# Two-layer graph attention on one core: raw weights of the pair scheme loaded one superblock sooner, raw-block sums on VectorE, fewer asides per pair, contexts of blocks 14 and 15 moved

## The chip, the cores and the metric

The kernel runs on one core of a Trainium2 chip. The metric is the device time of one execution in microseconds, the median of several runs. The engines are TensorE (PE in the profile, with its weight loads as PEld), VectorE (DVE), ScalarE (ACT), GpSimd (POOL) and SyncE (SP), which here issues nearly all DMAs. Each engine takes its instructions in program order and waits on semaphores.

## The reference, cut to what matters

The input is x of 128 graphs with 64 nodes and 768 features, and an adjacency of 128 x 64 x 64. All is float32.

```
h = max(layernorm(x), 0)
for l in 0, 1:
    u_left, u_right = h (W_left[l] h)^T / sqrt(768),  h (W_right[l] h)^T / sqrt(768)
    u = u_left on and above the diagonal, u_right below it (masked by the adjacency)
    att = exp(u) * adj, normalized over each row
    ctx = att @ (h W_lin[l]^T + b_lin[l])
    h = relu(layer_norm(ctx) * ln_a[l] + ln_b[l])
out = x + h
```

## The kernel before

**Tiling.** The 8192 rows are 16 blocks of 512 rows (8 graphs). Two blocks make a superblock, of which there are 8 (`NU`). A weight of 768 x 768 is cut into 3 x 3 raw blocks of 256 x 256, each one tile of 128 x 512 floats (256 KB). Products are not made block by block: a fast scheme for block matrices makes sums of raw weight blocks and sums of token blocks, multiplies those, and adds the results into the output blocks. For a superblock this scheme has 29 products instead of 36 (`PRODUCTS` for left and right weights, `PAIRS` for W_lin of layer 0). Its 23 weight sums stand in `W_OPS`; 9 of them have two raw blocks as operands (numbers below 9), the rest need other sums, two are sign changes. An older scheme with 15 products for a single block (`W_SUMS`, 17 weight sums, made in place from the raw blocks; `ORDER`) still serves the last two blocks of layer 0 and all of layer 1.

**Stages.** For each layer, `pass_one` makes the left and right products, scores and softmax (8 superblocks); `pass_two` makes the W_lin products (in layer 0: 7 superblocks by `pair`, then blocks 14 and 15 by `linear`, the last one in two halves), and from them and the softmax the contexts (`context`, `finish`). In the profile, pass one of layer 0 ends at about 901 us, the seven pairs run from 904 to 1305 us, blocks 14 and 15 until 1378 us.

**Order by hand.** There is no scheduler. `put(slot, f)` hangs work of the other engines on a numbered slot between TensorE's groups of matmuls: in pass one every product has four slots (116 in a superblock), in a pair two (58). `run(slot)` issues what hangs on a slot, and one item of the queue `idle`, the asides: only where nothing was given for the slot, or in every case where its second argument is true. `None` in `idle` is an empty place.

**The weights of the pair scheme** are made in the last superblock of pass one of layer 0 (there `run` takes an aside in each slot). `one_aside(0)` puts in order: 10 empty places, 9 loads of raw W_lin blocks (`load_n`: each load is led by a one-column marker, `paced`, a memset on DVE, which holds it until the tile is free), the centring of the blocks on DVE (`centre`), and `pair_weights`: 9 stores of raw blocks to memory (`keep`), 23 sums, which alternate between POOL and DVE, each with its store, then the 17 sums of the old scheme on POOL with stores, and the first 9 loads of streamed weights (`stream_n`). All this lies in one area of SBUF, `room`; sums whose last reader is done give their tile to a later sum. A pair's weight load is issued nine products ahead.

**The asides of pass two of layer 0** (`two_aside`) load the raw left and right blocks of layer 1, sum them on POOL and store them, in the shares that `pair` gives: for products with an odd number in both slots whatever is given, for even ones only in slots with nothing given.

**End of the pairs.** In the last pair `first_weights` loads the first six weights of the old scheme into the tile `xb` at slot 30. In `linear`, `ends` says behind which step of a block a context is made and in which slots its inverse and its two scalings follow (the scalings free the two PSUM banks `aux` for the next context).

**SP's queue** holds loads and stores of all kinds in program order; a store that waits for a sum holds all that stands behind it. The program numbers its DMAs around eight semaphores, so that a DMA waits for the one eight before it.

Of the kernel before, what the change touches and what calls it, by code (L numbers as in the profile page):

```python
# [17 lines left out]
def kernel(  # L18
# [12 lines left out]
    nc = tc.nc  # L31
# [70 lines left out]
    W = {}  # L102
# [158 lines left out]
    def pair_weights(own):  # L261

        where = {3 * i + j: single(s) for s, (i, j) in RAW.items()}
        spare = deque([single(s) for s in range(len(ORDER)) if s not in RAW] + own)
        last = {}
        for n, (_, o, _, a, b) in enumerate(W_OPS):
            for w in (a, b, o):
                last[w] = n

        def keep(w):  # L270
            if w in WN:
                nc.sync.dma_start(WN[w], where[w])

        def sums(n, eng):
            _, o, sign, a, b = W_OPS[n]
            t = where[o] = spare.popleft()
            if sign == "neg":
                eng.tensor_scalar_mul(t, where[a], -1.0)
            else:
                added(eng, t, sign, where[a], where[b])  # L280
            keep(o)
            for w in sorted({a, b, o}):
                if w >= 9 and last[w] == n:
                    spare.append(where[w])

        for w in range(9):
            idle.append(lambda w=w: keep(w))
        for n in range(len(W_OPS)):
            idle.append(lambda n=n: sums(n, (nc.gpsimd, nc.vector)[n % 2]))
        final = {s: -1 for s in range(len(ORDER))}  # L290
        for n, (o, *_) in enumerate(W_SUMS):
            final[o] = n

        def old(n):
            o, s, a, b = W_SUMS[n]
            added(nc.gpsimd, single(o), s, single(a), single(b))
            keep_old(n)

        def keep_old(n):
            for s in final:  # L300
                if final[s] == n:
                    nc.sync.dma_start(WO[s], single(s))

        idle.append(lambda: keep_old(-1))
        for n in range(len(W_SUMS)):
            idle.extend([lambda n=n: old(n), None])
        idle.append(None)
        for n in range(NR):
            idle.append(lambda n=n: stream_n(n))
# [634 lines left out]
    def pass_two(l, aside):  # L944
        last = l == L - 1
        with (tc.tile_pool(name=f"ps_two{l}", bufs=1, space=bass.MemoryType.PSUM) as ps,
# [154 lines left out]
            def pair(s, ends):  # L1101

                late, seen, bank = [], set(), {}
                HL[2 * s] = new_hl(2 * s)
                if not s:
                    HL[1] = new_hl(1)
                for i, (w, t, at, new, what) in enumerate(PAIRS):
                    if new:
                        bank[at] = ps_st.tile([P, 2 * TH], F32, name=at)
                    p = bank[at].rearrange("p (r d) -> p r d", r=2)  # L1110
                    x, wt = tokens(l, s, t, 2), single((s * len(PAIRS) + i) % NR)
                    for r in range(2):
                        for c in range(K2):
                            nc.tensor.matmul(p[:, r], x[:, c, r * P:(r + 1) * P], wt[:, c, :],  # L1114
                                             start=(new and r == c == 0), stop=(c == K2 - 1), skip_group_check=True)
                        if r == 0:
                            run(2 * i, i % 2)
                    now, late = late + [(p, what[n], int(what[n + 1], 16)) for n in range(0, len(what), 2)], []
                    for pp, sign, o in now:
                        u, j = 2 * s + o % 4 // 2, o // 4  # L1120
                        if u not in HL:
                            late.append((pp, sign, o))
                            continue
                        to = HL[u][:, o % 2 * 2:o % 2 * 2 + 2, j * D:(j + 1) * D]
                        if o in seen:
                            added(nc.vector, to, sign, to, pp)
                        else:
                            read_biased(pp, to, sign, j)
                        seen.add(o)
                    for o, last_i in LAST_PAIR.items():  # L1130
                        if last_i == i and o >= 12:
                            free((2, l, s, o))
                    n = s * len(PAIRS) + i + NR
                    if n < (NU - 1) * len(PAIRS):
                        stream_n(n)
                    else:
                        k = n - (NU - 1) * len(PAIRS)
                        nc.sync.dma_start(single(n % NR), WO[ORDER[6 + k][0]])
                        W[l, "n"][ORDER[6 + k][0]] = single(n % NR)
                    if i == 27 and s == NU - 2:  # L1140
                        AHEAD.append(fresh(l, 0, (0, 1)))
                    if i in ends:
                        what, slots = ends[i]
                        for f, n in zip(finish(*what), slots):
                            put(n, f)
                        if what[1] and what[0] == 2 * s - 2:
                            HL[2 * s + 1] = new_hl(2 * s + 1)
                    run(2 * i + 1, i % 2)
                assert not late

            def first_weights():
                t = sp.tile([P, H // 32, Q, 32], F32, name="xb", bufs=1).rearrange("p b q j -> p (b q j)")
                W[l, "n"] = {}
                for n in range(6):
                    to = W[l, "n"][ORDER[n][0]] = t[:, n * K2 * D:(n + 1) * K2 * D].rearrange("p (c d) -> p c d", c=K2)
                    nc.sync.dma_start(to, WO[ORDER[n][0]])

            def pairs():
                for s in range(NU - 1):
                    for n in range(2):  # L1160
                        put(4 + 10 * n, lambda n=n: load_h(2, l, 2 * s + 2 + n))
                        put(40 + 3 * n, lambda n=n: load_at(2 * s + n))
                    put_pair_ops(s, "after", PAIR_SLOTS)
                    if s + 1 < NU - 1:
                        put_pair_ops(s + 1, "before", PAIR_SLOTS)
                    else:
                        put_sums_t((2, l, NB - 2), 52, 1, 37)
                    for u, slot in ((NB - 5, 29), (NB - 4, 0)):
                        if u // 2 == s:
                            put(slot, lambda u=u: load_rows(1, u + 5 - NB, sp))  # L1170
                            put(slot + 1, lambda u=u, slot=slot: put_all(
                                slot + 14, transpose_rows(1, u + 5 - NB, sp), 1))
                    if s == NU - 2:
                        put(30, first_weights)
                    if s in aside:
                        aside[s]()
                    ends = {}
                    if s:
                        ends = {e: ((2 * s - 2 + n // 2, n % 2), (2 * e + 6, 2 * e + 7, 2 * e + 8))
                                for n, e in enumerate((0, 4, 9, 14))}  # L1180
                    pair(s, ends)
                    for n in sorted(plan):
                        plan[n - PAIR_SLOTS] = plan.pop(n)
                return NB - 2
# [35 lines left out]
            for u in range(0 if last else pairs(), NB):  # L1220
                turn = not last and u >= NB - 2
                put(12 if turn and u == NB - 2 else 4, lambda u=u: load_at(u))
                if u + 1 < NB:
# [9 lines left out]
                        aside[u]()  # L1233
                    ends = {}
                    if not last:
                        ends = {4 * n: ((u - 2 + n // 2, n % 2), (8 * n + 6, 8 * n + 7, 8 * n + 8)) for n in range(4)}
                    elif u:
                        ends = {0: ((u - 1, 0), (6, 7, 8, 11, 12)), 7: ((u - 1, 1), (20, 21, 22, 30, 30))}
                    linear(u, (0, 1), 0, ends, (0, 1) if u + 2 < NB else (0,))
# [2 lines left out]
                else:  # L1242
                    if turn:
                        put_token_ops(1, 0, "before")
                        assert not idle, len(idle)
                        for n in range(RINGS - 1):
                            put(20 + 4 * n, lambda n=n: stream(1, n))
                        ends = ({1: ((u - 1, 0), (13, 14, 16)), 11: ((u - 1, 1), (34, 35, 36))},
                                {4: ((u, 0), (50, 51, 52))})
                    else:  # L1250
                        last_block(u)
# [10 lines left out]
    def bias_aside(l):  # L1262
        def begin(sp):
            rows["bias", l] = bias(l)
        return begin

    def one_aside(l):
        def begin(sp):
            idle.extend(none * (8 if l else 10))
            later(load_n(l), 0)  # L1270
            centre(l)
            if l:
                later(sums_n(l), 0)
            else:
                own = sp.tile([P, 2 * H], F32, name="own", bufs=1)
                pair_weights([own[:, n * K2 * D:(n + 1) * K2 * D].rearrange("p (c d) -> p c d", c=K2) for n in range(3)])
# [60 lines left out]
```

## Time and profile before

| what | value |
|---|---|
| median of 3 runs | 2730.79 us (2730.25 to 2731.34) |
| the profiled execution | 2728.26 us, its span 2726.1 us |
| mean granted TensorE clock | 0.996 |
| TensorE matmul busy | 2682.3 us, 98% |
| VectorE, ScalarE, GpSimd busy | 1575.3, 746.2, 1465.9 us |
| DMA | 636.25 MB, mean 233 GB/s |

The profile gives for each instruction its start and duration in microseconds from the start of the span, and for the idle time before it the event that ended it. In a timeline, neighbouring instructions of one kind are one row with their number (x8). A row of a window gives the stretch, its length, the busy time of PE, PEld, DVE, ACT and POOL with the number of instructions, the granted TensorE clock, the busy share of the 16 DMA engines and GB/s.

### The profile page before, as it was taken

How to read it: one execution, taken by the hardware profiler on the slowest of the kernel's cores; microseconds unless marked ns; L12 is line 12 of the kernel's file. 1: busy time of each engine (PE TensorE's matmuls, PEld its weight loads, DVE VectorE, ACT ScalarE, POOL GpSimd, SP SyncE). 2: the span in 40 equal slices, each digit the busy share in tenths (PEclk: the TensorE clock that was granted, in tenths of full speed). 3: DMA queues.
4: the chain of work that ended last, by engine and by line, in shares of the span. 5: the costliest groups of instructions: out<-in, count | busy, mean ns of one | idle time of the engine just before them, and what ended most of it. 6: DMA issues, size and time to landing. Idle time of an engine off the chain costs nothing.

```text
span 2726.1 us, 47585 instructions
## 1 busy us (share of the span) xinstructions
PE 2682.3 (98%) x18458; PEld 2293.3 (84%) x18458; DVE 1575.3 (58%) x2575; ACT 746.2 (27%) x1334; POOL 1465.9 (54%) x1139
## 2 busy tenths in 40 slices
PE   9999999999998999999999999999999999999998
PEld 7888888888887888887688888888888888888886
DVE  7664655756747655555334645545446476666667
ACT  4032131231310022222531221221212204444443
POOL 5633244244337899766443335334243286887886
PEclk9999999999999999999999999999999999999999
DMA  8886966867768799879685967859659534655655
GB/s 269 269 309 207 297 200 210 274 202 242 257 219 292 258 340 351 314 248 302 207 267 181 301 208 241 247 202 301 201 194 313 196 101 126 179 160 163 177 161 149
DMA packets 347807, 636.25 MB, mean 233 GB/s; under 512 B 67008, under 2 KB 194240, under 8 KB 339392
## 3 DMA queue, kind: packets, MB, share of 16 engines
q1 hardware_dynamic: 347424, 632.82, 71.5%
q8 instruction: 148, 2.42, 0.4%
q14 instruction: 75, 0.61, 0.1%
q10 hardware_dynamic: 160, 0.39, 0.0%
HBM read 486.55 MB, written 146.54 MB: 232 GB/s over the span
## 4 chain that ended last, share of the span: by engine, by line
PE 90%; DVE 2%; POOL 2%; DMA 2%; issue 1%; ACT 1%; SPq 0%; DVEq 0%; POOLq 0%; ACTq 0%
PE right L628 16%; PE X L628 10%; PE V L628 10%; PE Z L628 8%; PE Y L628 8%; PE X L1200 7%; PE both L567 4%; PE V L1200 4%; PE Y L1114 3%; PE aux L974 3%; PE X L1114 3%; PE Y L1200 3%; PE Z L1114 3%; PE V L1114 3%; PE Z L1200 2%; POOL room L247 1%
## 5 line engine op out<-in xcount | busy, mean ns | idle before, releaser
L247 POOL TENSOR_TENSOR ts<-ht 128x512 f32<-128x512 f32 x303 | 418.1, 1385 | 103.1 <-PE right L628 48.5
L247 POOL TENSOR_TENSOR ts<-ht,ts 128x512 f32<-128x512 f32 x192 | 253.1, 1327 | 308.4 <-PE V L628 197.9
L628 PE MATMUL right<-ts,wp 128*128 128x252 f32 (+1 forms) x1632 | 381.2, 377 | 2.4 <-DVE m L247 1.8
L628 PEld LDWEIGHTS right<-ts,wp 128*128 128x128 f32 x1632 | 309.8, 190 | 42.2 <-DVE m L247 2.8
L247 POOL TENSOR_TENSOR ts<-ht,ht 128x512 f32<-128x512 f32 x191 | 243.8, 1284 | 170.9 <-PE right L628 92.7
L576 POOL TENSOR_TENSOR wm<-adj,tri 128x256 f32<-128x256 f32 x60 | 42.8, 735 | 476.2 <-DMA wp<-ws 370.0
L247 DVE TENSOR_TENSOR m<-m,X 128x512 f32<-128x512 f32 x160 | 105.4, 684 | 254.7 <-ACT m L398 166.3
L247 DVE TENSOR_TENSOR m<-m,right 128x504 f32<-128x504 f32 (+1 forms) x304 | 199.3, 673 | 86.6 <-PE right L628 73.6
L628 PE MATMUL Z<-ts,wp 128*128 128x256 f32 x992 | 234.4, 379 | 1.0 <-POOL room L247 1.0
L628 PEld LDWEIGHTS Z<-ts,wp 128*128 128x128 f32 x992 | 188.3, 190 | 26.2 <-POOL room L247 1.4
L628 PE MATMUL X<-ts,wp 128*128 128x256 f32 x872 | 207.5, 381 | 1.0 <-DVE wp L247 1.0
L628 PE MATMUL V<-ts,wp 128*128 128x252 f32 (+1 forms) x864 | 201.7, 377 | 0.0
L628 PEld LDWEIGHTS X<-ts,wp 128*128 128x128 f32 x872 | 164.4, 190 | 24.6 <-POOL ts L247 1.3
L628 PEld LDWEIGHTS V<-ts,wp 128*128 128x128 f32 x864 | 164.1, 190 | 20.8 <-DVE m L247 0.4
L475 ACT ACTIVATE ht<-ht,b_col,a_col 128x512 f32<-128x512 f32 x192 | 140.7, 803 | 138.6 <-DMA ht<-h 138.6
L398 ACT ACTIVATE m<-right 128x504 f32<-128x504 f32 (+1 forms) x64 | 36.1, 590 | 504.2 <-PE both L567 484.1
L1054 ACT ACTIVATE z<-aux 128x768 f32<-128x768 f32 x126 | 101.0, 807 | 230.8 <-PE aux L974 214.5
L1067 POOL TENSOR_TENSOR z<-z,b 128x768 f32<-128x768 f32 x62 | 112.7, 1830 | 89.8 <-DVE z L1064 89.8
L247 DVE TENSOR_TENSOR m<-m,Y 128x512 f32<-128x512 f32 x144 | 95.7, 683 | 109.8 <-PE Y L628 99.6
L247 POOL TENSOR_TENSOR ts<-ts,ht 128x512 f32<-128x512 f32 x110 | 141.5, 1287 | 13.8 <-PE V L628 8.3
L628 PE MATMUL right<-ht,wp 128*128 128x252 f32 (+1 forms) x624 | 146.2, 378 | 0.0
L247 DVE TENSOR_TENSOR m<-m,V 128x504 f32<-128x504 f32 (+1 forms) x160 | 104.4, 677 | 71.9 <-PE V L628 60.8
(264 smaller groups left out, 5128.3 us busy)
## 6 DMA issues: line engine op xcount, KB each, us to landing
wp<-ws SPq DMA_DIRECT2D x435, 512.0 KB, 6.3
ht<-h SPq DMA_DIRECT2D x62, 1536.0 KB, 8.5
room<-wn SPq DMA_DIRECT2D x203, 256.0 KB, 4.8
h<-room SPq DMA_DIRECT2D x112, 384.0 KB, 6.9
z<-z SPq DMA_DIRECT2D x128, 192.0 KB, 4.8
ws<-wp SPq DMA_DIRECT2D x93, 256.0 KB, 4.9
xr<-in_x_dram SPq DMA_DIRECT2D x120, 192.0 KB, 3.7
out_dram<-xr SPq DMA_DIRECT2D x120, 192.0 KB, 2.6
```

The lines of the kernel that those rows point to most:

```text
L247: (eng.tensor_add if sign == "+" else eng.tensor_sub)(o, a, b)
L398: nc.scalar.activation(to(o), p, AF.Copy, scale=1.0 if sign == "+" else -1.0)
L475: nc.scalar.activation(ht, ht, AF.Relu, bias=cols[1][:, c:c + 1], scale=cols[0][:, c:c + 1])
L567: nc.tensor.matmul(p[h * S + e:h * S + e + 32, q, e:e + 95], ht[:, c, b * S + e:b * S + e + 32], mb[:, e:e + 95], start=(c == 0), stop=(c ...
L576: nc.gpsimd.tensor_tensor(wm[:, :, k], adj[:, :, 1 - k], tri[:, k].unsqueeze(1).to_broadcast([P, Q, S]), op=ALU.mult)
L628: nc.tensor.matmul(p[:, g], wk[:, c, g * P:(g + 1) * P], tk[:, c, :].rearrange("p (b s) -> p b s", s=S)[:, :, :ns], start=(new and g == c ...
L974: nc.tensor.matmul(cx[k][i, m, :HH], at[j, q, :], hl[j, q, m * HH:(m + 1) * HH], start=True, stop=True)
L1054: nc.scalar.activation(zs[k].rearrange(two, n=2), cx[k], AF.Square, accum_out=ss[:, k:k + 1])
L1067: nc.gpsimd.tensor_add(zs[k], zs[k], rows["b"])
L1114: nc.tensor.matmul(p[:, r], x[:, c, r * P:(r + 1) * P], wt[:, c, :], start=(new and r == c == 0), stop=(c == K2 - 1), skip_group_check=True)
L1200: nc.tensor.matmul(p[:, n], b[t][:, c, r * P:(r + 1) * P], w[s][:, c, :], start=(i in FIRST and i not in PRELOAD and n == c == 0), stop=(c ...
```

## The change

1. The nine raw loads leave `one_aside(0)` and are put, one per slot, on slots 99 to 107 of the superblock before (`bias_aside`); the ten empty places go.
2. Of the 23 weight sums, the 9 with two raw operands go to DVE and the other 14 to POOL, each of the latter with an empty place behind it.
3. In a pair, every product gives an aside its second slot in any case, and its first slot if nothing is given there.
4. `first_weights` goes from slot 30 to slot 44 of the last pair; the dictionary it fills is made earlier.
5. In blocks 14 and 15: the inverse and the scalings of a context in block 14 come one slot sooner; in block 15 the context of the first half of block 14 is made behind step 3, not step 1, with its inverse and scalings four slots later.

```
@@ pair_weights
         for n in range(len(W_OPS)):
-            idle.append(lambda n=n: sums(n, (nc.gpsimd, nc.vector)[n % 2]))
+            raw = W_OPS[n][2] != "neg" and max(W_OPS[n][3:]) < 9
+            idle.append(lambda n=n, raw=raw: sums(n, nc.vector if raw else nc.gpsimd))
+            idle.extend(none * (not raw))
@@ pair
                         if r == 0:
-                            run(2 * i, i % 2)
+                            run(2 * i)
...
-                    run(2 * i + 1, i % 2)
+                    run(2 * i + 1, True)
@@ first_weights
-                W[l, "n"] = {}
@@ pairs
                     if s == NU - 2:
-                        put(30, first_weights)
+                        W[l, "n"] = {}
+                        put(44, first_weights)
@@ pass_two, blocks 14 and 15 of layer 0
-                        ends = {4 * n: ((u - 2 + n // 2, n % 2), (8 * n + 6, 8 * n + 7, 8 * n + 8)) for n in range(4)}
+                        ends = {4 * n: ((u - 2 + n // 2, n % 2), (8 * n + 5, 8 * n + 6, 8 * n + 7)) for n in range(4)}
...
-                        ends = ({1: ((u - 1, 0), (13, 14, 16)), 11: ((u - 1, 1), (34, 35, 36))},
+                        ends = ({3: ((u - 1, 0), (17, 18, 20)), 11: ((u - 1, 1), (34, 35, 36))},
                                 {4: ((u, 0), (50, 51, 52))})
@@ bias_aside
             rows["bias", l] = bias(l)
+            if l == 0:
+                put(98, lambda: put_all(99, load_n(l)))
@@ one_aside
-            idle.extend(none * (8 if l else 10))
-            later(load_n(l), 0)
+            if l:
+                idle.extend(none * 8)
+                later(load_n(l), 0)
             centre(l)
```

## The prediction

> **What bounds the kernel now.** I read the page's busy table first, then the waits of TensorE by stretch, then the timelines of TensorE, VectorE (DVE), GpSimd (POOL) and SyncE (SP) around each stretch that has waits.
>
> ```profile
> PE 2682.3 (98%) x18458; PEld 2293.3 (84%) x18458; DVE 1575.3 (58%) x2575; ACT 746.2 (27%) x1334; POOL 1465.9 (54%) x1139
> ```
>
> TensorE is the bound: 43.8 us of the 2726.1 us span are not matmul. From 160 to 795, 960 to 1270 and 1380 to 2240 us it hardly waits. So the change can give only what TensorE loses at the end of the first attention pass, the start and end of the pair stage, and the two linear blocks behind it.
>
> ```profile
> 846.71 3.25 PE L628 MATMUL Y<-ht,wp 128*128 128x256 f32 x8 [2.46 <-DVE m L247]
> 849.75 2.37 PE L628 MATMUL right<-ht,wp 128*128 128x256 f32 x8
> 903.94 2.40 PE L1114 MATMUL X<-room,ht 128*128 128x256 f32 x8 [2.42 <-DMA room<-wn]
> 906.13 3.19 PE L1114 MATMUL Y<-room,ht 128*128 128x256 f32 x8
> 936.11 1.99 PE L1114 MATMUL Y<-room,ht 128*128 128x256 f32 x8 [1.73 <-DMA room<-wn]
> 1286.20 2.37 PE L1114 MATMUL Z<-room,ht 128*128 128x256 f32 x8 [2.69 <-DMA room<-wn]
> 1296.86 1.97 PE L1114 MATMUL Y<-room,ts 128*128 128x256 f32 x8 [1.83 <-DMA room<-wn]
> 1326.51 1.51 PE L974 MATMUL aux<-hl,at 64*64 64x384 f32 x12 [0.63 <-ACT z L1072]
> ```
>
> Columns: start, length, instruction, idle time before it. An undisturbed group of eight matmuls starts 1.7275 us after the last (799.11 to 809.47: six groups in 10.36). I count what a stretch loses as its starts against this step, since a wait also slows what follows:
>
> ```profile
> 846.00:850.00 4.00, 3.29 (x9) 2.70 (x10) 2.33 (x4) 0.00 (x0) 4.00 (x3) 0.66 0.77 251
> 904.00:907.00 3.00, 3.00 (x11) 2.49 (x12) 2.86 (x5) 0.00 (x0) 2.92 (x3) 0.72 0.89 308
> 936.00:940.00 4.00, 3.89 (x18) 3.46 (x19) 1.42 (x3) 0.00 (x0) 2.13 (x3) 1.00 0.64 169
> ```
>
> The third number from the end is the granted clock: 0.66 and 0.72 behind waits of 2.46 and 2.42 us, 1.00 behind one of 1.73. So a wait above some 2.4 us costs about 1.8 more (846.71: 3.25-1.89 and 2.37-1.89; 903.94: 0.46+1.29 over the step). The Trainium skill, page "TensorE: Matmul & The Clock Gate", section "The HAM clock gate", puts the drop only behind an idle window of about 3.4 us. By that none of these waits would carry a surcharge, and some 5 us of the losses below would be unexplained. The rows decide.
>
> The losses: **A**, last superblock of pass one: 49 steps from 795.65 to 890.65 take 95.0 us where 84.65 are due, 10.35 lost. **B**, first pair: 2.42+0.46+1.29 at the start, 0.9 at 925, 2.0 at 936. **C**, last pair: 4.6 around 1286, 2.06 at 1296. **D**, blocks 14 and 15: 2.01 at 1325, 1.99 at 1335.6, 1.75 at 1344.8, 1.32 at 1365.3.
>
> **Part 1, loads a superblock sooner, raw sums on DVE (A).** The cause of A is order, not load:
>
> ```profile
> 829.31 1.27 POOL L247 TENSOR_TENSOR room<-room 128x512 f32<-128x512 f32 x1 [21.78 <-DVE room L243]
> 842.92 1.74 DVE L247 TENSOR_TENSOR room<-room 128x512 f32<-128x512 f32 x1 [3.74 <-POOL room L247]
> 885.32 14.26 SPq L302 DMA_DIRECT2D wo<-room x6
> 899.63 5.79 SPq L259 DMA_DIRECT2D room<-wn x9
> ```
>
> POOL sits 21.8 us behind the centring on DVE, because the W_lin blocks land only at 808 to 812. Then DVE and POOL wait for each other through sums that alternate, with the token sums and the reads of PSUM queued behind. After the change the nine loads are issued at slots 99 to 107 of the superblock before, about 758 to 766, where SP is nearly empty. Their 2.3 MB delay ring loads of 512 KB that are issued five to eight products (17 to 27 us) before use, which hides it. The nine markers on DVE before them wait for the store of block 15, issued 745.6 to 750 and landed 6.9 later, by 757: some 0 to 0.5. Centring moves into 773 to 806, where DVE now idles 15.6 us. The nine raw sums depend on no sum of POOL. The other fourteen go to POOL, one per two slots: two more there, two fewer on DVE. With the empty places added and dropped, the asides of this superblock are 116 for 116 slots instead of 121, so the first loads of the pair stage are issued at slots 107 to 115 rather than partly after the last product; they wait for POOL's sums in either case, and cost nothing of their own.
>
> Is POOL fast enough? Slot s of this superblock lies at 781.7+0.864s. Its first sum is slot 35, 812. From there to its last old sum (slot 104) stand 50 adds and 2 masks. At 1.27 (alone) this ends at 877, at 1.45 for the 27 adds that share time with DVE sums at 882. It lags its slots by 5 to 10 us; token sums are issued 16 slots (13.8 us) ahead, so TensorE waits 0 to 2. DVE's sums take 1.592 at the median beside POOL (0.65 at least). Four of them between slots 57 and 60 are 6.4 us, and they reuse tiles whose stores land at about 831 to 834.5, just when needed: 0 to 1 of wait. I take 8.5 of 10.35 back, with ends of 6 and 10.3.
>
> A rule speaks against this part: the Trainium skill, "SBUF — State Buffer", section "Who interferes with whom", says that a DVE instruction with two SBUF inputs blocks against a POOL instruction that reads SBUF. The 1.592 agrees. If every POOL op paid 1.72 by it, the 50 would end at 899 and A would return nothing. The sum goes by 1.27 to 1.45, since after slot 61 DVE has only PSUM reads left.
>
> **Part 1 at the start of the pairs (B).** Scores end at 901.5 now, 891 to 895 after. The nine first weights are issued behind the last old sum (now 899.6, landed 903.8; nine issues take 5.8): after 877 to 882 they land between 881 and 892, so the 4.2 lost at 903.94 goes. But what follows hangs on another clock, which the change leaves as it is: DVE's softmax of block 14 ends 6.4 after the scores, eight att stores take 5.1 of SP, and only then comes the tenth weight (913.18). With DVE free of POOL it would be 4.9. The twelfth weight is queued behind a 1.5 MB token load and lands 11 us after the tenth is issued (3.0 MB now, 2.75 after, one raw load fewer in front): 21 to 22.7 after the scores, against 23.7 now, where TensorE would want it at 19.2. Step 16 likewise: 31.5 to 33 against 34.5. So B returns 1.0 to 3.5 of 7.1, mostly as waits below 2.4; I take 2.0.
>
> **Part 2, fewer asides per pair.** Loads, sums and stores of the layer-1 weights spread: stores end at pair step 121, not 97; the right raw loads move from steps 53 to 58 to steps 63 to 71, behind two token loads and among z stores. DMA is full there (0.97 to 1.06 busy from 1012 to 1070). Weight loads land with little to spare: step 8's of pair 2 at 1049.6 for a use at 1051.27. One or two 256 KB loads more in front (0.7 each at 360 GB/s) make waits of 0 to 1.5; elsewhere the pressure falls. I take 0.6 lost, ends 0 and 4.
>
> Stores and sums of the asides go to SP and POOL alone there, POOL being 82% busy (255 of 310 us), so nothing on TensorE's path waits for them but the weight loads.
>
> **Part 3, first linear weights at slot 44 (C).** Now six loads go out at 1287.85 for 3.04 us of SP, ahead of the weight issued 1290.99 that ends the 1.83 wait. Moved, that weight goes 3 us sooner: 2.06 gone. The 4.6 around 1286 stays: that weight was issued at 1279.81, before the six. They now go at about 1295.4, 4 to 8.8 to land, for a use at 1303.5: 0 to 0.7. C returns 1.3 to 2.1; I take 2.0.
>
> **Part 4, contexts (D).** One slot sooner lets the first scaling on ACT pass one PSUM read: the second scaling ends 0.76 sooner before 1325 and 0.75 before 1335 (its VectorE inverse doesn't move). In block 15 the context goes behind step 3, but the scaling now stands ahead of the read of X that step 2 needs: that read ends at 1344.6 to 1345.1 against 1343.8 wanted, so 0.9 to 1.3 lost for 1.75. D returns 0.5 to 3; I take 2.1.
>
> The dictionary made earlier is no instruction.
>
> **Sum.** 8.5+2.0-0.6+2.0+2.1 = 14.0. The profiled run took 2728.26 (span plus 2.2), 2.5 below the median of 2730.79; the saving is taken from the median: 2716.8.
>
> **Rivals.**
> 1. The stall moves: DVE waits for recycled tiles and POOL lags to 899. A returns 5, B 1.0, C 2, D 0.5, pairs lose 1: 7.5, 2723.3. For it: the stores land when needed. Against: POOL starts 17 us sooner.
> 2. Everything goes, the pair start too: A 10.3, B 7.1, C 2.1, D 4.5: 24, 2706.8. Against: the token load in the queue.
> 3. The other side: the weight stream in pairs 2 to 4 falls behind. A weight over 2.4 late costs the wait and 1.8 of clock, 4.2 or more. Five such places undo 20 and give 2730.8-14.6+21 = 2737. It decides from loads landing 4 us later than now (1.7 spare plus 2.4). For it: DMA full. Against: the bytes are the same and pair 1, with as many stores, has no wait today. A milder form, two or three places, gives 2725 to 2731.
> 4. The loads don't come sooner: excluded by the order of the queue, where they stand among ring loads 2 to 4 of the next superblock; C, D and the pairs' loss alone would give 2727.3.
>
> **Chances.** Forecast 0.60 (2711 to 2721), rival 1 0.15, rival 2 0.07, rival 3 0.16 (0.06 of it slower), rival 4 0.02. Same means within 0.2%, 2725.3 to 2736.3, which is about what a measurement can tell. Faster 0.83, same 0.11, slower 0.06. The range takes in rival 1 and the near ends of 2 and 3.
>
> **What would show it.** Right: room loads landed by 776; no POOL wait of 20 us in 800 to 830; the old sums done by 882; no TensorE wait on DVE m above 1 us in the last superblock; at the pair start no wait for step 0, but one of 1 to 2.4 us around steps 11 and 16; no wait before 1297's step; 1286's still there. Wrong: a POOL chain to 899, waits on wn in pairs 2 to 4, or a wait of the first linear steps on xb.

## The result and the profile after

The changed kernel takes 2722.8 us (median of 10 runs, 2721.65 to 2728.35) against 2731.18 for the kernel before beside it: a ratio of 0.9971, 95% interval 0.9962 to 0.9981. That is 7.9 us less (5.2 to 10.4). The forecast was 14.0 less, and its first rival 7.5. The profiled execution took 2723.55 us, its span 2721.7.

The busy table of the page after:

```profile
PE 2680.5 (98%) x18458; PEld 2294.8 (84%) x18458; DVE 1575.1 (58%) x2573; ACT 745.8 (27%) x1334; POOL 1468.3 (54%) x1141
```

TensorE's timeline after, those rows that have a wait of 0.4 us or more between 790 and 1350 us (start, length, instruction, idle time and what ended it):

```profile
847.13 3.68 PE L630 MATMUL Y<-ht,wp 128*128 128x256 f32 x8 [4.50 <-DVE m L247]
898.94 2.48 PE L569 MATMUL Z<-m,ht 128*32 128x95 f32 x108 [2.00 <-issue]
924.57 2.69 PE L1116 MATMUL Z<-room,ts 128*128 128x256 f32 x8 [3.24 <-DMA room<-wn]
1284.02 1.96 PE L1116 MATMUL Z<-room,ht 128*128 128x256 f32 x8 [1.46 <-DMA room<-wn]
1288.97 1.97 PE L1116 MATMUL X<-room,ht 128*128 128x256 f32 x8 [1.26 <-DMA room<-wn]
1321.36 1.51 PE L976 MATMUL aux<-hl,at 64*64 64x384 f32 x12 [0.43 <-ACT z L1074]
1331.19 1.51 PE L976 MATMUL aux<-hl,at 64*64 64x384 f32 x12 [0.43 <-ACT z L1074]
1339.34 1.10 PE L1202 MATMUL X<-xb,ts 128*128 128x256 f32 x4 [1.27 <-ACT hl L400]
1345.22 1.10 PE L1202 MATMUL X<-room,ts 128*128 128x256 f32 x4 [0.55 <-ACT hl L400]
```

The last superblock (A) is left with one wait. It is longer than any before, and with the slower clock behind it A still loses 6.4 us. The start of the pairs has no wait for its first weight any more, but in the scores before it a wait of 2.00 us stands instead of 0.66, and the one at step 11 grew from 0.35 to 3.24. These two rows before:

```profile
899.04 2.48 PE L567 MATMUL Z<-m,ht 128*32 128x95 f32 x108 [0.66 <-issue]
925.21 1.97 PE L1114 MATMUL Z<-room,ts 128*128 128x256 f32 x8 [0.35 <-DMA room<-wn]
```

The wait in front of 1297's step is gone. The contexts of block 14 wait 0.43 instead of 0.63, and their four-matmul groups no longer wait.

To set the terms of the forecast against the traces I cut the span at points that both kernels have: the first group behind the second scores of the last superblock (t0), the start of its final scores, the first context of the second pair, the first linear step, and the first group of layer 1.

| stretch, us | before | after | saved | forecast |
|---|---|---|---|---|
| A: last superblock from t0 | 100.37 | 96.44 | 3.9 | 8.5 |
| final scores and first pair | 68.01 | 68.78 | -0.8 | 2.0 |
| other pairs | 345.09 | 341.90 | 3.2 | 1.4 |
| blocks 14 and 15 | 73.12 | 72.31 | 0.8 | 2.1 |
| sum | | | 7.2 | 14.0 |

The rest of the span is 2.8 longer in the execution after: 1.9 of it before t0, 0.9 behind the last stretch, where the change does nothing. The nine raw loads now lie before t0, but they are no clear price: t0 is 791.1 to 796.6 in the eight traces with early loads, and 792.1 to 794.9 in the four without.

**Where A's wait comes from.** By "the rings" I mean the 16 DMA engines with what is queued for them; how busy they are stands in the rows of a window. SP's queue after the change, around the wait, two rows of it:

```profile
824.48 1.24 SPq L470 DMA_DIRECT2D ht<-h  x1
829.62 0.32 SPq L272 DMA_DIRECT2D wn<-own  x1
```

and the chain of waits after the change, traced back from the end of this stretch (start, length, what):

```profile
829.62 10.71 DMA wn<-own
840.33 0.03 issue
840.36 0.02 DVEq L247
840.38 0.04 issue
840.42 4.39 DVE own L247 x3
844.81 1.67 DVE room L247
846.48 0.61 DVE m L247
847.09 0.04 issue
847.13 3.68 PE Y L630 x8
```

The first row of the queue is a token load of 1.5 MB, put on slot 40 of this superblock. The store of a weight sum, 256 KB, is issued 5 us behind it and lands 10.7 us after its own issue, at 840.3. Only then may DVE overwrite the tile with its next raw sum. Four such sums then follow without a gap, 6.1 us, and behind them stands the read of PSUM that TensorE needs.

### The profile page after: what moved, and what is told of

It is laid out like the page before. It is cut to its first block, busy times and chain, and to the rows that moved or that the text cites. A ratio compares the mean times of both kernels' runs of the same rounds, so it can differ in the third digit from the quotient of the medians.

```text
span 2721.7 us, 47573 instructions
## 1 busy us (share of the span) xinstructions
PE 2680.5 (98%) x18458; PEld 2294.8 (84%) x18458; DVE 1575.1 (58%) x2573; ACT 745.8 (27%) x1334; POOL 1468.3 (54%) x1141
## 3 DMA queue, kind: packets, MB, share of 16 engines
q8 instruction: 148, 2.42, 0.4%
## 4 chain that ended last, share of the span: by engine, by line
PE 93%; DVE 1%; DMA 1%; issue 1%; ACT 1%; SPq 0%; POOL 0%; DVEq 0%; POOLq 0%; ACTq 0%
PE right L630 17%; PE X L630 11%; PE V L630 10%; PE Z L630 9%; PE Y L630 9%; PE X L1202 7%; PE both L569 5%; PE V L1202 4%; PE X L1116 4%; PE Y L1116 4%; PE aux L976 3%; PE Y L1202 3%; PE Z L1116 3%; PE V L1116 3%; PE Z L1202 2%
## 5 line engine op out<-in xcount | busy, mean ns | idle before, releaser
L247 POOL TENSOR_TENSOR ts<-ts,ht 128x512 f32<-128x512 f32 x110 | 142.6, 1297 | 13.9 <-PE V L630 8.4
```

The costliest lines, as they stand in the source:

```text
L247: (eng.tensor_add if sign == "+" else eng.tensor_sub)(o, a, b)
```

## The experiments

Times are medians beside the kernel before on the same chip (2732.7 us in the first four runs, 2731.98 in the next four, 2731.82 in the last two). Part 1 to part 4 are the parts as the prediction numbers them.

**1. The second token load later (late_token).** The changed kernel with

```
-                        put(12 + 28 * n, lambda n=n: load_h(2, l, n))
+                        put(12 + (28 if l else 64) * n, lambda n=n: load_h(2, l, n))
```

> The changed kernel with one edit: in the last superblock of pass one of layer 0 the 1.5 MB token load of block 1 for the pair stage is issued at slot 76 instead of 40. Theory: the 4.5 us wait of TensorE at 847 us comes from this load, which stands in SP's queue and in the DMA rings ahead of the stores that DVE's raw sums wait for (store issued 829.6, landed 840.3). Then that wait and the 1.8 us of low clock behind it go, the stretch loses under 1 us instead of 6.4, and the time is 6 us below the changed kernel's 2722.8: 2715.5 to 2718. Rival: DVE is late because its sums share time with POOL (1.2 to 1.7 us each instead of 0.65) and pile up between slots 54 and 61; then a wait on DVE m of over 2.4 us stays and the time is above 2720.

2720.23 us, ratio 0.9952 (0.9938 to 0.9965). TensorE's timeline:

```profile
839.97 1.99 PE L630 MATMUL Y<-ht,wp 128*128 128x256 f32 x8 [0.28 <-DVE m L247]
889.16 2.48 PE L569 MATMUL Z<-m,ht 128*32 128x95 f32 x108 [1.64 <-issue]
```

The wait is 0.28 instead of 4.50, and A takes 90.52 us instead of 96.44: of the 10.35 us that A lost before, 9.85 are back. The stores of sums now land within 6.2 us at the most. The token load in front of them was the cause: the wait was 0.28 and 0.30 in the two traces with this edit (runs 1 and 10), and 2.19 to 5.20 in the four without it (the changed kernel and runs 5, 6 and 7). By the two ratios it is 0.19%, 5.2 us, faster than the changed kernel, near the 5.9 us that A returns between the two traces, though the two intervals just overlap.

**2. Part 1 alone (p1_only).** The kernel before with the hunks of `pair_weights`, `bias_aside` and `one_aside`, and nothing else of the change.

> The kernel before with part 1 alone (loads one superblock sooner, raw sums on DVE, empty places). Theory by the trace of the changed kernel: the last superblock loses 6.4 us instead of 10.35, the pair start gains 1, the final scores lose up to 1.9 more: 1 to 5 us below before's 2731.2, so 2726 to 2730; the last pair loses 6.7 as before. Rival: part 1 is what also shortened the wait near 1286 us (4.6 to 3.2), then that wait is 3.2 here.

2727.36 us, ratio 0.998 (0.9972 to 0.9989).

```profile
847.11 1.99 PE L630 MATMUL Y<-ht,wp 128*128 128x256 f32 x8 [2.83 <-DVE m L247]
896.66 2.48 PE L569 MATMUL Z<-m,ht 128*32 128x95 f32 x108 [2.00 <-issue]
923.41 3.50 PE L1116 MATMUL Z<-room,ts 128*128 128x256 f32 x8 [3.04 <-DMA room<-wn]
1295.12 3.16 PE L1116 MATMUL Y<-room,ts 128*128 128x256 f32 x8 [2.62 <-DMA room<-wn]
```

A saves 7.3 us here (93.08), so it loses 3.1 where 6.4 was expected. The wait in the scores, the one at step 11 and the one in A are all there, so they belong to part 1. The wait near 1297 stays, so its end is not part 1's doing; run 7 ties it to part 3.

**3. The earlier loads alone (loads_only).** As 2, without the `pair_weights` hunk: the sums alternate between POOL and DVE as before.

> The kernel before with the nine raw loads one superblock sooner, the sums alternating between POOL and DVE as before and without empty places. If the alternation is the cause of the waits, DVE and POOL go on waiting for each other and the stretch loses 6 to 10 us; time 2727 to 2731. Rival: the late loads alone were the cause; then the stretch loses under 4 us and this is as fast as part 1 as a whole or faster.

2732.61 us, ratio 1.0004 (0.9995 to 1.0012). TensorE's timeline has five waits in the last superblock; three of them:

```profile
834.63 1.97 PE L628 MATMUL Y<-ts,wp 128*128 128x256 f32 x8 [3.16 <-issue]
844.04 1.97 PE L628 MATMUL Z<-ts,wp 128*128 128x256 f32 x8 [2.03 <-POOL room L247]
874.23 3.68 PE L628 MATMUL Z<-ts,wp 128*128 128x256 f32 x8 [2.86 <-POOL ts L247]
```

A takes 103.63 us, 3.3 more than before: it loses 13.6 where 6 to 10 was expected. Raw blocks that are there earlier bring nothing while two engines take turns in one chain of sums; on top of them, the split by operands with its empty places is what pays. The split without the earlier loads was not run.

**4. All but part 1 (without_p1).** The changed kernel with those three hunks taken back.

> The changed kernel with part 1 undone (loads, alternation and empty places as before). Theory: the stretch to 892 us loses 10.35 as before, the last pair 3.2 instead of 6.7, blocks 14 and 15 1 us less than before: 2731.2-3.5-1.0 = 2726.7. Rival: the asides given out more slowly cost by themselves in the first pair or later, then 2729 or more; or the shorter wait near 1286 us needs part 1, then 2728.

2728.04 us, ratio 0.9983 (0.9975 to 0.9992). A is 100.54 and scores with first pair 67.53, as before; pairs 1 to 6 save 1.7 and the linear blocks 0.8. The pairs give 1.8 less than the 3.5 expected: around 1286 4.7 us are lost here, as before. The rival said 2728, because the shorter wait there needs part 1. That stays open: in the seven traces with the whole of part 1 the loss there is 3.2 to 5.1. This run and run 2 together save 0.37%, against 0.29% for the whole, with overlapping intervals, so nothing speaks against the parts simply adding.

**5. The first pair's token loads later (late_pair).** The changed kernel with

```
-                        put(4 + 10 * n, lambda n=n: load_h(2, l, 2 * s + 2 + n))
+                        put((4 if s else 24) + 10 * n, lambda n=n: load_h(2, l, 2 * s + 2 + n))
```

> The changed kernel with one edit: the first pair's two token loads (1.5 MB each, for the blocks of the second pair) go out at slots 24 and 34 instead of 4 and 14. Theory: the 3.24 us wait in front of step 11 of the first pair is there because the twelfth weight is queued behind the first of these loads; with the load gone from in front of it the wait ends or falls below 1 us, and with it the 2 us of lower clock behind it. Scores and first pair take 64 to 66 us instead of 68.8, and the time is 2718 to 2720. Rival: DVE's softmax of block 14 and the eight att stores set when the weight is issued, whatever is ahead of it in the rings. Then 2 us or more of wait stay at step 11, and the time stays at 2722 to 2724. A second rival: the wait only moves to where the token loads stand now, near steps 16 to 24; then step 11 is free and a wait of 2 us or more stands there, at 2721 to 2724.

2720.34 us, ratio 0.9954 (0.9939 to 0.9969). Step 11 has no wait any more, and scores and first pair take 64.69 us instead of 68.78. TensorE's rows that still wait for a pair weight:

```profile
942.07 1.97 PE L1116 MATMUL V<-room,ts 128*128 128x256 f32 x8 [0.73 <-DMA room<-wn]
1284.83 1.97 PE L1116 MATMUL Z<-room,ht 128*128 128x256 f32 x8 [3.41 <-DMA room<-wn]
1289.73 1.97 PE L1116 MATMUL X<-room,ht 128*128 128x256 f32 x8 [1.21 <-DMA room<-wn]
```

By the ratios this is 0.17%, 4.6 us, faster than the changed kernel, with intervals that overlap; the traces differ by 4.1 in this stretch. So the 1.5 MB load in front of the twelfth weight was the cause, not DVE's softmax or the att stores. The wait at 1284 is 3.41 instead of 1.46; it was 2.79 in run 6, where nothing up to that point differs from the changed kernel, so its size changes from execution to execution and is no price of this edit.

**6. Block 15's context back behind step 1 (old15).** The changed kernel with

```
-                        ends = ({3: ((u - 1, 0), (17, 18, 20)), 11: ((u - 1, 1), (34, 35, 36))},
+                        ends = ({1: ((u - 1, 0), (13, 14, 16)), 11: ((u - 1, 1), (34, 35, 36))},
```

> The changed kernel with one edit: the first context of block 15 back behind step 1, where it was before (the scaling slots 13, 14 and 16 again); the contexts of block 14 stay one slot sooner. Theory: the move in block 15 was no gain: it took one wait of 1.75 us away and put two in its place (behind the read of X of step 2 and of step 4 on ACT) that lose 2.2. So undoing it gives 0.4 to 0.6 us back, in the linear blocks alone: 71.8 instead of 72.3 us from the first linear step to the second layer. Rival, as the prediction had it: the move is worth 0.5 to 0.9, and the linear blocks take 72.8 to 73.2.

2725.44 us, ratio 0.9971 (0.9961 to 0.9981), the same as the changed kernel's. TensorE's timeline at this place:

```profile
1342.44 0.86 PE L976 MATMUL aux<-room,at 64*64 64x384 f32 x4 [0.90 <-ACT z L1074]
1343.82 1.51 PE L976 MATMUL aux<-room,at 64*64 64x384 f32 x12 [0.51 <-ACT z L1074]
```

The linear blocks take 72.28 us, against 72.31 with the move. Both readings were wrong: the move takes away 1.41 us of waits for ACT's scaling and brings 1.82 for ACT's reads of X, and the end of the blocks does not move.

**7. The first linear weights at slot 30 (fw30).** The changed kernel with `put(30, first_weights)` for `put(44, first_weights)`.

> The changed kernel with one edit: the six first linear weights go out at slot 30 of the last pair again, as before, instead of 44. Theory: the wait of 1.8 us near 1297 comes back, because the six issues take 3 us of SP ahead of the weight that this step needs; pairs 1 to 6 take 343.7 to 344.5 us instead of 341.9, and the time is 2 us longer, 2724 to 2725.5. Rival: the wait near 1297 went because the weights as a whole come sooner after the rest of the change; then pairs 1 to 6 stay within 0.5 us of 341.9.

2725.89 us, ratio 0.9977 (0.9965 to 0.9988), so 1.6 us slower than the change by the ratios, with intervals that overlap. The trace is plainer:

```profile
843.16 1.99 PE L630 MATMUL Y<-ht,wp 128*128 128x256 f32 x8 [2.19 <-DVE m L247]
1280.21 2.43 PE L1116 MATMUL Z<-room,ht 128*128 128x256 f32 x8 [2.37 <-DMA room<-wn]
1290.76 1.96 PE L1116 MATMUL Y<-room,ts 128*128 128x256 f32 x8 [1.72 <-DMA room<-wn]
```

The wait in front of the step that stood at 1297 is back with 1.72 us, and pairs 1 to 6 take 345.68 instead of 341.90 (341.90 to 344.13 in the five traces with `first_weights` at slot 44 and the rest of the change). The edit acts on the last pair alone, yet A took 92.43 us here, with a wait of 2.19, against 95.93 to 97.12 with waits of 3.99 to 5.20 in the changed kernel and runs 5 and 6. Up to this place the four execute the same instructions, so A's wait too changes by 3 us between executions: it ends with the landing behind the token load.

**8 and 9. What the wait in the final scores hangs on (dma_full, dma_scores).** The wait "issue" in front of the Z products of the final scores was 0.66 before and 2.00 after. The kernel before got copies of 1.5 MB within device memory, which feed nothing. Run 8:

```
+                        copies = [dram.tile([P, C, T], F32, name=f"copy{n}") for n in range(2)]
+                        for n in range(2):
+                            put(SLOTS - 1, lambda n=n: nc.scalar.dma_start(copies[n], KEPT[l][n]))
```

> The kernel before with one addition: two copies of 1.5 MB from device memory to device memory are issued on ACT's queue at the last slot of the last superblock, so that the rings are full while the final scores of pass one run. They feed nothing. It tells what the wait in front of the final scores' Z products (issue, 0.66 us before the change and 2.0 after it) hangs on. Theory: an instruction load is queued in the same rings behind data, so the wait grows with data in flight, to 1.4 us or more. Rival: it has to do with the order of instructions in the changed kernel; then the wait stays below 0.9 here. The time grows in any case, by 2 to 12 us, since the first pair's weights are behind the 3 MB.

2737.96 us. Nothing held ACT's queue back, and the copies were issued at 834 us and had landed by 848.3, so they fell into A, which took 106.66 us. TensorE's timeline in the final scores:

```profile
903.23 1.97 PE L567 MATMUL Z<-m,ht 128*32 128x95 f32 x84
905.36 2.48 PE L567 MATMUL Z<-m,ht 128*32 128x95 f32 x108 [0.17 <-issue]
```

The 16 DMA engines were 0.03 to 0.34 busy from 898 to 908, and the wait 0.17. The run could not tell. In run 9 the copies follow the last five old sums on SP's queue:

```
             keep_old(n)
+            if n >= len(W_SUMS) - 5:
+                nc.sync.dma_start(dram.tile([P, C, T], F32, name=f"copy{n}"), KEPT[0][n % 4])
```

> The kernel before with five copies of 1.5 MB from device memory to device memory on SP's queue, one behind each of the last five sums of the old weights, so that the rings are full from about 887 us through the final scores (in the run with two copies on ACT's queue they had ended before, at 860 or so: that run could not tell). They feed nothing. Theory: an instruction load of TensorE, 16 KB on a queue of its own, shares the rings with this data; the wait put down to issue in front of the final scores' Z products, 0.66 us before the change and 2.0 after it, then grows to 2 us or more here, with the order of TensorE's instructions as before. Rival: the wait belongs to the order of the changed kernel, and stays below 0.9. The time grows by 10 to 25 us in any case, since the first pair's weights stand behind the copies.

2743.78 us, one execution. TensorE's timeline, and then two windows of it (granted clock, DMA share and GB/s are the last three numbers):

```profile
905.14 1.96 PE L569 MATMUL both<-m,ht 128*32 128x95 f32 x42 [4.75 <-issue]
913.53 3.98 PE L569 MATMUL Z<-m,ht 128*32 128x95 f32 x108 [3.32 <-issue]
```

```profile
900.40:905.10 4.70, 0.00 (x0) 0.00 (x0) 0.00 (x0) 0.00 (x0) 4.62 (x5) 0.78 0.94 321
909.50:913.50 4.00, 0.71 (x24) 0.54 (x17) 1.46 (x2) 0.42 (x1) 3.83 (x3) 0.93 1.03 367
```

With the order of TensorE's instructions as before, the wait grew from 0.66 to 3.32, and a second one of 4.75 came up in front of the last left and right scores. So it comes from data in the rings and not from the changed order. The trace has two packets of 16 KB on a queue of its own for instructions between 900 and 915 us, and by time they go with the waits: one ends at 903.70 and one at 912.22, and TensorE goes on at 905.14 and 913.53. It is the same in the other traces: such a packet ends at 897.78 before the change, at 897.49 after it and at 903.92 in run 8, and the wait ends 1.3 to 1.5 us behind it, at 899.04, 898.94 and 905.36. That these packets are the code TensorE waits for is the reading that fits; no semaphore shows it. After the change the rings are full here (0.89 to 1.04 busy from 890 to 896, against 0.00 to 0.20 before) because the nine first weights are issued at 888.5 and not at 899.6, and fall into the scores. The Trainium skill, "Runtime: NRT & Kernel Launch", section "Instruction fetch mechanics", has an engine fetch its code in blocks of 16 KiB over a DMA queue of its own, at a cost that is mostly hidden. The packets of 16 KB agree; in these final scores the cost is not hidden, if the reading is right.

**10. Both token loads out of the way (both_late).** The edits of 1 and 5 together.

> The changed kernel with both token loads out of the way: the second load of the last superblock at slot 76 instead of 40, and those of the first pair at slots 24 and 34 instead of 4 and 14. Theory: the two waits (4.5 us in the last superblock, 3.24 us at step 11 of the first pair) have causes of their own, so the gains add: about 90.5 us for the last superblock, 64.7 to 65.5 for scores and first pair, and 2715 to 2718 us in all, 5 to 8 below the changed kernel. Rival: what is gained early is handed on and lost again where the DMA rings are full, in the last pair (its waits were 1.46 and 1.26 us in the changed kernel, and 3.41 and 1.21 with the first pair's loads later); then pairs 1 to 6 take 344 to 347 us instead of 341.9, and the time is 2718 to 2721.

2715.52 us (2714.64 to 2717.62), ratio 0.9943 (0.993 to 0.9957): 15.6 us below the kernel before, about twice what the change brings, and below both kernels.

```profile
844.11 1.99 PE L630 MATMUL Y<-ht,wp 128*128 128x256 f32 x8 [0.30 <-DVE m L247]
893.17 2.48 PE L569 MATMUL Z<-m,ht 128*32 128x95 f32 x108 [1.51 <-issue]
904.62 1.96 PE L1116 MATMUL Y<-room,ts 128*128 128x256 f32 x8 [1.87 <-issue]
935.52 1.97 PE L1116 MATMUL V<-room,ts 128*128 128x256 f32 x8 [1.31 <-DMA room<-wn]
1276.96 1.97 PE L1116 MATMUL Z<-room,ht 128*128 128x256 f32 x8 [2.12 <-DMA room<-wn]
1281.70 1.97 PE L1116 MATMUL X<-room,ht 128*128 128x256 f32 x8 [1.05 <-DMA room<-wn]
```

A takes 90.56 us, scores and first pair 65.48, pairs 1 to 6 342.64. The gains of the two stretches add in the traces, and the pairs take 0.7 more than in the changed kernel, no more than executions differ by. By the ratios the two edits bring 0.28% together, and 0.19% and 0.17% singly, which agrees within the intervals. The wait at 904.62 (0 to 1.96 us in the runs) is of another kind than the one in the scores: the rings are 0.00 to 0.04 busy from 896 to 904, and the chain of waits runs through five token sums of POOL without a gap, until 903.24. It ends 1.38 us behind the last of these sums, and so it does in runs 1, 2 and 7 (1.38 or 1.39). That ties it to POOL; no row fills the 1.38 us, and no run tried it.

## Why the prediction was right, and where it was wrong

The direction held, and so did the range, which took in the first rival; the likeliest case, 2711 to 2721 at a chance of 0.60, did not: 14.0 was forecast and 7.9 came. What happened is nearest to the first rival, in which DVE waits for tiles whose stores have not landed (7.5 in all, at a chance of 0.15). That its sum comes so near is in part luck: it has B at 1.0 returned, where 0.8 was lost, and the last pair with the other pairs at 1.0, where 3.2 came.

- **A, 8.5 forecast, 3.9 in this trace** (3.3 to 7.9 in the four traces that are alike up to here). The step that failed: "they reuse tiles whose stores land at about 831 to 834.5, just when needed: 0 to 1 of wait". The store landed at 840.3. I had priced it like a store in quiet rings and had not put the 1.5 MB token load of slot 40, issued 5 us ahead of it, into the queue. Without that load A returns 9.85 (run 1), so the rest of the step, and POOL's pace, were good (the last old sum ended at 880.9 there). The first rival's other half, POOL lagging to 899, did not come: the last old sum ended at 888.1. That is six later than the 882 I gave, with t0 1.9 later in this execution and 4.4 us of POOL waiting before the masks. That row names a store, but POOL's sequencer went on at 837.57, when an adjacency load had landed (837.54), which was issued 2.0 us behind the same 1.5 MB token load.
- **The loads.** The raw loads were issued from 765.8 to 775.2 us with 6.2 us to land, not at 758 to 766, and POOL waited 25.5 us for its first sum, until 815.4 instead of 812. I had listed a long POOL wait there as a sign against me. It costs TensorE nothing, since its place is before 815 and TensorE has no wait there.
- **B, 2.0 forecast, -0.8 measured.** "The 4.2 lost at 903.94 goes" was right: the first weights wait no more. Step 11 was named as the next place, with 21 to 22.7 us after the scores for the twelfth weight. It came at 23.1 (924.44 after 901.35), so the term was mis-sized by 0.4 us or more, and the wait of 3.24 fell where the clock drops. Runs 5 and 10 show the token load as the cause. Step 16 has no wait. Unforeseen was the wait in the scores, 2.00 for 0.66: issuing the nine weights sooner puts their 2.3 MB into the stretch in which, by the reading of run 9, TensorE waits for its code.
- **Pairs, 0.6 lost forecast.** No wait of 0.3 us or more came up in pairs 2 to 6 in any run with fewer asides per pair, so the third rival is out, and this edit brought and cost nothing that can be seen. It was not run alone.
- **C, 2.0 forecast, 3.2 in this trace.** Part 3 did what was said (run 7). The rest lies around 1284, where I said that 4.6 stays: this wait has 1.46 to 3.41 us in executions of the changed kernel and its variants, and this trace caught a short one.
- **D, 2.1 forecast, 0.8 measured.** Block 14's two contexts returned 0.72 and 0.71 as worked out (0.76 and 0.75). In block 15 I counted one read of X held up by ACT's scaling, 0.9 to 1.3. There are two, of 1.27 and 0.55, and undoing the move changes nothing (run 6). With either order block 15 takes 40.8 us from behind the last of these contexts, against 40.2 before, so 0.6 of what block 14 returned is lost again; why it is with the old order too was not tried.
- **The surcharge of the clock.** "A wait above some 2.4 us costs about 1.8 more" was read from three rows, and is no rule (below).

## What to carry to other kernels

When a sum may only start once the store of its tile has landed, price the landing by the bytes that stand ahead of it in the rings at that moment, not by a store's usual time: the 256 KB of a sum took 10.7 us here behind 1.5 MB, and at most 6.2 in run 1, without it. Large loads that are needed late belong behind the small transfers that someone waits for; moving three token loads to later slots gave about as much again as the whole change. And a change that issues its loads earlier should be followed to what else uses the rings in that stretch, code included if the reading of run 9 is right.

## What the runs showed of the hardware

**The clock drop behind a wait is not set by the length of the wait alone.** Windows behind waits of three kernels; the third number from the end is the granted clock. The changed kernel behind 4.50 us, then behind 3.24 us:

```profile
847.10:850.80 3.70, 3.67 (x9) 3.02 (x10) 2.96 (x5) 0.00 (x0) 3.61 (x4) 0.54 0.84 283
924.50:929.00 4.50, 4.43 (x13) 3.62 (x14) 0.69 (x1) 0.00 (x0) 1.26 (x1) 0.63 1.08 398
```

Run 5 (late_pair) behind 3.41 us:

```profile
1284.80:1286.60 1.80, 1.77 (x8) 1.62 (x9) 0.00 (x0) 0.00 (x0) 1.35 (x2) 1.00 0.91 283
1286.60:1288.40 1.80, 1.80 (x9) 1.34 (x8) 1.28 (x2) 0.00 (x0) 0.00 (x0) 1.00 0.91 228
```

Run 2 (p1_only) behind 2.83 us:

```profile
847.10:849.00 1.90, 1.89 (x9) 1.69 (x10) 1.90 (x4) 0.00 (x0) 1.81 (x3) 1.00 0.97 333
849.00:851.00 2.00, 2.00 (x11) 1.77 (x10) 2.00 (x4) 0.00 (x0) 2.00 (x2) 1.00 0.92 297
```

Waits of 2.42 and 2.46 us had a drop in the kernel before, while 2.83 and 3.41 had none. So between about 2.4 and 3.4 us it is open whether a wait costs some 1.8 us more. The Trainium skill, "TensorE: Matmul & The Clock Gate", section "The HAM clock gate", says that the window of about 3.4 us in which activity is watched runs freely, so that it depends on where in the window work falls. That agrees with a drop for some waits and not for others of the same length; that an idle window must be a full 3.4 us does not agree with the drops behind 2.42 and 2.46.

**Waits of TensorE in the final scores grow with the data in the rings.** They are put down to issue: 3.32 and 4.75 us with the rings 0.94 to 1.03 busy, against 0.17 and 0.66 where they were at most 0.38 busy, each ending 1.3 to 1.5 us behind a 16 KB packet of instructions. Not every wait put down to issue is of this kind: the 1.87 us in run 10 came with the rings empty, behind POOL's sums.
